# Where the layer norms and their transposes stand in a cross-attention block on one NeuronCore

## The chip, the cores and the metric

The kernel runs on one core of one Trainium2 chip. The metric is the time on the device in microseconds (us), as the median of several runs. Besides these runs there is one execution under the hardware profiler; it has a time of its own, and every duration below is from it.

## What is computed

A cross-attention block in float32: four batches, 512 query rows (`x`) and 512 encoder rows (`ctx`) of 512 features each, 16 heads of 32 features, an MLP of 2048. The mask is all ones.

```python
x = layer_norm(hidden_states, ln1_w, ln1_b)          # (4, 512, 512)
q = x @ q_w + q_b                                    # 16 heads of 32
k = encoder @ k_w + k_b
v = encoder @ v_w + v_b
attn = softmax(where(mask, q k^T / sqrt(32), min))
hidden = (attn v) @ cproj_w + cproj_b + residual
y = gelu(layer_norm(hidden, ln2_w, ln2_b) @ fc_w + fc_b, approximate=True)
out = hidden + y @ proj_w + proj_b
```

## The kernel before

Work is in groups. A group `w` from 0 to 15 is one batch (`w // 4`) and four of its heads (`w % 4`), because four heads of 32 features fill 128 partitions. For a group three products are prepared: K and Q as `[features, rows]` (`prep_k` L196, `prep_q` L206) and V as `[rows, features]` (`prep_v` L218). Each is 4 or 16 matmuls into one PSUM accumulator and a copy out of it by ScalarE (L198, L209, L223); POOL then adds V's bias (L230). After its matmuls each of the three asks for the weights of the group two further on (`load_w`, L189).

Then the group is passed through in four units of 128 query rows. A unit is `scores` (L240, four matmuls into the only `sc` buffer[...]), on VectorE (DVE) a copy with the mask that also takes the minimum (L245), on ScalarE (ACT) the exponential (L249), and `turn`: DVE transposes the exponentials in 32x32 blocks into `tb` (L277). After every second unit DVE appends the reciprocal sums (L282 to L285), and `copies` (L319) moves the 16 blocks of `tb` between partitions by 16 DMAs: this is the exchange, named by group and half. Its target is `pT`, of which there is one, or for some halves the large tiles `gt` or `xe` while they are free. `attend` (L362, `av`) multiplies the exchanged exponentials by V, two or three units after they were made, and DVE divides by the sums into `oT` (L367).

Other tiles matter to the order. `xe` holds a batch's encoder rows (`eT`, loaded by `load_enc`, L150) and its normed and transposed query rows (`xT`). There is one of it, so the next batch's encoder rows can be loaded only when the last V of the batch before has been taken, and `xT` can be overwritten only when its last Q has been. A layer norm is in parts: `x1` loads the rows, `x2` is three parts (statistics of tiles 0 and 1, L116 and L117; of tiles 2 and 3, with the reciprocal root on POOL, L122 and L124; the norm of all four tiles, L128), `x3` is four transposes of the normed tiles through TensorE (L137) with a copy that applies weight and bias, on ACT for even ones (L142) and on DVE for odd ones (L140). `x4` is `load_enc`. The second norm has the same parts (`stat`, `rs`, `norm`, `turns2`). Four accumulators of PSUM (`ps_acc`) are shared by every product, transposes and `av` among them.

The order of all instructions is written out by hand. `first[w]` is a list of pieces of work for group `w`, `later[w]` what may follow from its third unit on. `A(w)` gives the K, Q and V pieces of a group, `C(b)` the output projections (L399), `some(n)` the next n products of the MLP (fc L457, proj L467). The loop over units lays them out by a budget: each piece has a cost (3.4 for a product, 0.5 for a transpose, 0 for the rest), the sum of the group is divided by its four units, and before and after each unit's `turn` as many pieces are taken as the budget allows. So the position of a piece in a list doesn't fix the unit that it falls in, and a pair of transposes can be parted by a unit's scores. Nearly all DMAs, the exchanges among them, are issued by SyncE (SP) in the same order. An issue whose source isn't ready holds back everything that stands behind it.

The last two MLPs have a form of their own (`last_mlps`), which comes after all that is touched here.

Of the kernel before, what the change touches and what calls it, by code (L numbers as in the profile page):

```python
# [74 lines left out]
def xattn_block(ctx: ExitStack, tc: tile.TileContext, x, encT, mask, q_w, k_w, v_w, c_w, fc_w, p_w, vecs, rows, out):  # L75
# [43 lines left out]
    def ln_rs(key):  # L119

        ve = small.tile([P, NT], F32, tag="ve", name=f"ve{key[0]}_{key[1]}")
        nc.gpsimd.tensor_scalar(ve, S["mv", key][:, :, 1], EPS, 1.0, ALU.add, ALU.mult)  # L122
        rs = small.tile([P, NT], F32, tag="rs", name=f"rs{key[0]}_{key[1]}")
        nc.gpsimd.tensor_tensor(rs, ve, nhalf, ALU.pow)  # L124
        S["rs", key] = rs
# [65 lines left out]
    def prep_k(w):  # L191
        b, g = divmod(w, NG)
        kT = kqp.tile([P, L], F32, tag="kT", name=f"kT_{w}")
        acc = acc_tile(f"acck_{w}")
        for d in range(ND):
            nc.tensor.matmul(acc, S["wk", w][:, d, :], eT[:, d, :], start=(d == 0), stop=(d == ND - 1))  # L196
        load_w(w + 2, names=("wk",))
        nc.scalar.activation(kT, acc, AF.Identity, bias=vec[:, KB + g : KB + g + 1], scale=1.0)  # L198
        S["kT", w] = kT

    def prep_q(w):
        b, g = divmod(w, NG)
        qT = kqp.tile([P, L], F32, tag="qT", name=f"qT_{w}")
        acc = acc_tile(f"accq_{w}")
        for d in range(ND):
            nc.tensor.matmul(acc, S["wq", w][:, d, :], xT[:, d, :], start=(d == 0), stop=(d == ND - 1))  # L206
        load_w(w + 2, names=("wq",))

        nc.scalar.activation(qT, acc, AF.Identity, bias=qb[:, g : g + 1], scale=-scale)  # L209
        S["qT", w] = qT  # L210

    def prep_v(w):
        b = w // NG
        v = five.tile([P, NT, P], F32, tag="v", name=f"v_{w}")
        acc = acc_tile(f"accv_{w}")
        for t in range(NT):
            for d in range(ND):
                nc.tensor.matmul(  # L218
                    acc[:, ts(t, P)], eT[:, d, ts(t, P)], S["wv", w][:, d, :],
                    start=(d == 0), stop=(d == ND - 1),  # L220
                )
        load_w(w + 2, names=("wv",))
        nc.scalar.copy(v, acc.rearrange("p (t f) -> p t f", t=NT))  # L223
        S["v", w] = v
        if w:
            v_bias(w)
# [153 lines left out]
    def load_h(b, *ts_):  # L380

        if ("xa", b) not in S:
            S["xa", b] = dram.tile([L, D], F32, tag=f"xa{b}", name=f"xa{b}")
        for t in ts_:
            pool, tag = (hids, "hid") if stays(b, t) else (tiles, "xn")
            S["h", b, t] = pool.tile([P, D], F32, tag=tag, name=f"h_{b}_{t}")
            Q[0].dma_start(out=S["h", b, t], in_=x[b, ts(t, P), :])
            if stays(b, t):
                S["hid", b, t] = S["h", b, t]
# [23 lines left out]
    def stat2(b, t):  # L413
        ln_stat((2, b), t, S["h", b, t])

    def norm2(b, t):
        h = S["h", b, t]
        y = tiles.tile([P, D], F32, tag="xn", name=f"xn2_{b}_{t}") if stays(b, t) else h
        S.setdefault(("yn", b), {})[t] = y
        ln_norm((2, b), t, y, h)  # L420

    def proj_bias(b):
        for t in range(NT):
            if stays(b, t):
                add_row(S["hid", b, t], 1)
# [271 lines left out]
    def do(fn):  # L697
        return [(0.0, fn)]

    def A(w):  # L700
        if w >= NW:
            return []
        return [
            (CHAIN, lambda: prep_k(w)),
            (CHAIN, lambda: prep_q(w)),
            (CHAIN, lambda: prep_v(w)),
        ]

    def C(b):
        return [(CHAIN, lambda t=t: cproj(b, t)) for t in range(NT)]  # L710
# [4 lines left out]
    def turns2(b):  # L715
        return [(TURN, lambda d=d: ln2_turn(b, d)) for d in range(ND)]
# [7 lines left out]
    def inputs(b):  # L724
        ln = [(0.0, lambda part=part: ln1(b, part)) for part in range(3)]
        return do(lambda: load_x(b)), ln, turns1(b), do(lambda: load_enc(b))
# [44 lines left out]
    first = [[] for _ in range(NW)]  # L771
    later = [[] for _ in range(NW)]
    x1, x2, x3, x4 = inputs(1)
    k2, q2, v2 = A(2)
    k3, q3, v3 = A(3)
    k4, q4, v4 = A(4)
    first[0] = [(CHAIN, lambda: prep_v(1)), (CHAIN, lambda: prep_q(1))] + x1 + [k2, q2]
    first[1] = x2[:1] + [v2, k3] + x2[1:2] + [q3] + x2[2:] + [v3] + x4 + x3
    first[2] = [q4, k4, v4] + A(5)[:1]
    first[3] = A(5)[1:] + A(6)  # L780
    mlp = []
    for p in range(NORMAL):
# [2 lines left out]
    def some(n):  # L785
        taken, mlp[:n] = mlp[:n], []
        return taken
# [4 lines left out]
    def h_(b, *ts_):  # L792
        return do(lambda: load_h(b, *ts_))

    def cb(b):
        return do(lambda: c_bias(b))

    def pb_(b):
        return do(lambda: proj_bias(b))

    def rs(b):
        return do(lambda: ln_rs((2, b)))

    def stat(b, *ts_):
        return do(lambda: [stat2(b, t) for t in ts_])

    def norm(b, *ts_):
        return do(lambda: [norm2(b, t) for t in ts_])


    x1, x2, x3, x4 = inputs(2)
    first[3] = x1 + first[3] + cb(0)
    k, q, v = A(7)
    c, t2 = C(0), turns2(0)
    first[4] = [k] + x2[:2] + [q] + x2[2:] + [v] + x3[:2] + x4
    later[4] = c[:1] + x3[2:] + c[1:] + stat(0, 0, 1, 2, 3) + rs(0)
    k, q, v = A(8)
    first[5] = norm(0, 0, 1, 2, 3) + [q] + t2[:2] + [k] + t2[2:] + [v] + pb_(0) + some(5)
    k, q, v = A(9)
    x1, x2, x3, x4 = inputs(3)  # L820
    first[6] = [k, q] + some(5) + [v] + x1
    k, q, v = A(10)
    first[7] = [k, q] + some(6) + [v]

    k, q, v = A(11)
    first[8] = h_(1, 0, 1) + [k] + x2[:1] + [q] + x2[1:2] + some(1) + x2[2:] + [v] + x3 + h_(1, 2, 3) + x4
    later[8] = cb(1) + C(1)
    k, q, v = A(12)
    first[9] = [q] + some(2) + [k] + some(3) + [v]
    k, q, v = A(13)  # L830
    first[10] = [k, q] + some(5) + [v]
    k, q, v = A(14)
    t2 = turns2(1)
# [3 lines left out]
    k, q, v = A(15)  # L837
# [99 lines left out]
```

## Time and profile before

| | us |
|---|---|
| median of 3 runs | 843.63 (842.76 to 844.65) |
| the profiled execution | 839.66 |
| its span, first to last instruction | 837.9 |
| TensorE (PE) busy | 811.3 (97%) |
| DVE / ACT / POOL busy | 562.8 / 348.1 / 91.0 |
| mean granted TensorE clock | 0.986 |

Each row of the profile that is shown below names a line of the kernel, an engine, the operation, the tiles (out<-in), and how many instructions the row merges. In a timeline the first number is the start from the beginning of the span, the second the length, and brackets hold the idle time of the engine just before, with what ended it. In a row of waits the numbers are the total, the count and the longest. A row of a stretch has its ends, its length, the busy time of PE, of the weight loads (PEld), of DVE, ACT and POOL, then the granted clock (1.00 is full), the share of the DMA engines and GB/s. SPq is SyncE's queue of DMA issues.

### The profile page before, as it was taken

To read this page: it belongs to the slowest core of one execution; us is meant where nothing else is said; L and a number is where in the kernel's file an instruction comes from. 1 tells how busy PE (TensorE), PEld (TensorE's weight loads), DVE (VectorE), ACT (ScalarE), POOL (GpSimd) and SP (SyncE) were. 2 spreads that over 40 slices of the span, in tenths; PEclk is the share of its full clock that TensorE was granted. 3 is DMA by queue.
4 is the path that set the end of the run, shared out by engine and by line. 5 is a ranking of instruction groups with operands and counts; after the bars stand their busy time and mean duration, and the time that the engine had idled before them with its cause. 6 is when DMAs were issued, how large, how long until landed. Compare 5 with 4: busy or idle time off the path is not lost.

```text
span 837.9 us, 11898 instructions
## 1 busy us (share of the span) xinstructions
PE 811.3 (97%) x4020; PEld 468.9 (56%) x4020; DVE 562.8 (67%) x1264; ACT 348.1 (42%) x741; POOL 91.0 (11%) x98
## 2 busy tenths in 40 slices
PE   9997799889999998999999999999999999999998
PEld 6544445335445454454545445444446888888887
DVE  3699589685577587756787777688425988168511
ACT  2655364335665553355434657475401331023200
POOL 1010003002000012100012201001021003100011
PEclk9999899899999999999999999999999999999999
DMA  9667869845777775676676966677835551022001
GB/s 335 224 153 190 236 175 229 223 101 129 187 184 191 203 192 149 191 207 171 149 195 188 239 170 160 171 176 170 242 108 175 159 186 41 11 90 76 14 13 38
DMA packets 59740, 134.91 MB, mean 161 GB/s; under 512 B 12144, under 2 KB 14320, under 8 KB 59552
## 3 DMA queue, kind: packets, MB, share of 16 engines
q1 hardware_dynamic: 58416, 130.73, 57.7%
q0 software_dynamic: 736, 2.29, 0.8%
q10 hardware_dynamic: 528, 1.14, 0.5%
q8 instruction: 32, 0.52, 0.3%
q14 instruction: 28, 0.23, 0.1%
HBM read 58.74 MB, written 6.29 MB: 78 GB/s over the span
## 4 chain that ended last, share of the span: by engine, by line
PE 87%; DVE 8%; SPq 2%; DMA 2%; issue 1%; ACT 0%; POOL 0%; DVEq 0%; POOLq 0%; ACTq 0%
PE accf L457 13%; PE accp L467 13%; PE q L561 12%; PE sc L240 7%; PE accc L399 7%; PE av L362 6%; PE acck L196 6%; PE accv L218 5%; PE accq L206 4%; DVE tb L277 3%; DVE s L245 2%; SPq L319 2%; PE tp L137 2%; PE q4p L601 2%; PE q3p L601 2%; PE q5p L601 2%
## 5 line engine op out<-in xcount | busy, mean ns | idle before, releaser
L249 ACT ACTIVATE s<-s,mn 128x512 f32<-128x512 f32 x256 | 181.7, 711 | 143.6 <-DVE mn L245 143.4
L245 DVE CUSTOM_DVE_ANT_0 s<-sc,mb 128x512 f32<-128x512 f32 x256 | 161.4, 686 | 67.8 <-PE sc L240 67.6
L277 DVE STREAM_TRANSPOSE tb<-s 128x512 f32<-128x512 f32 x248 | 161.6, 690 | 8.5 <-ACT s L249 8.5
L457 PE MATMUL accf<-yT,fcw 128*128 128x512 f32 x256 | 115.2, 598 | 0.0
L467 PE MATMUL accp<-pw,gt 128*128 128x512 f32 x256 | 115.1, 599 | 0.0
L467 PEld LDWEIGHTS accp<-pw,gt 128*128 128x128 f32 x256 | 47.2, 190 | 64.5 <-issue 61.1
L457 PEld LDWEIGHTS accf<-yT,fcw 128*128 128x128 f32 x256 | 47.2, 190 | 64.5 <-issue 56.1
L240 PE MATMUL sc<-kT,qT 32*128 32x512 f32 x512 | 74.8, 655 | 2.0 <-DVE mn L245 1.3
L196 PE MATMUL acck<-xe,wk 128*128 128x512 f32 x128 | 61.6, 626 | 6.9 <-DMA xe<-encT_dram 6.9
L218 PEld LDWEIGHTS accv<-wv,xe 128*128 128x128 f32 x512 | 58.9, 192 | 9.4 <-issue 7.9
L218 PE MATMUL accv<-wv,xe 128*128 128x128 f32 x512 | 60.7, 277 | 0.2 <-ACT yT L142 0.2
L561 PE MATMUL q<-ys,gt 128*128 128x256 f32 x256 | 60.2, 379 | 0.0
L206 PE MATMUL accq<-xe,wq 128*128 128x512 f32 x128 | 59.1, 605 | 0.0
L399 PE MATMUL accc<-wc,oT 128*128 128x512 f32 x128 | 56.8, 596 | 0.0
L362 PE MATMUL av<-pT,v 128*32 128x256 f32 x864 | 55.0, 397 | 0.0
L561 PEld LDWEIGHTS q<-ys,gt 128*128 128x128 f32 x256 | 48.6, 190 | 6.6
L230 POOL TENSOR_TENSOR v<-v,row 128x512 f32<-128x512 f32 x16 | 20.3, 1272 | 293.4 <-ACT v L223 293.4
L249 ACT ACT_TABLE_LOAD x22 | 28.2, 1283 | 52.7 <-DVE mn L245 52.7
L249 ACT ACTIVATION_READ_ACCUMULATOR s<-s,mn 128x1 f32 x256 | 47.8, 187 | 0.0
L196 PEld LDWEIGHTS acck<-xe,wk 128*128 128x128 f32 x128 | 24.3, 200 | 40.6 <-issue 28.2
L561 PE MATMUL q<-yT,gt 128*128 128x256 f32 x192 | 46.3, 379 | 0.0
L362 PEld LDWEIGHTS av<-pT,v 128*32 128x32 f32 x864 | 26.0, 113 | 30.2 <-issue 13.3
(117 smaller groups left out, 844.8 us busy)
## 6 DMA issues: line engine op xcount, KB each, us to landing
pT<-tb SPq DMA_DIRECT2D x416, 136.0 KB, 2.4
fcw<-fc_w_dram SPq DMA_DIRECT2D x32, 256.0 KB, 3.1
pw<-p_w_dram SPq DMA_DIRECT2D x32, 256.0 KB, 4.7
gt<-fc_w_dram SPq DMA_DIRECT2D x32, 256.0 KB, 2.7
gt<-tb SPq DMA_DIRECT2D x48, 136.0 KB, 3.1
wk<-k_w_dram SPq DMA_DIRECT2D x16, 256.0 KB, 3.4
xe<-encT_dram SPq DMA_DIRECT2D x16, 256.0 KB, 4.5
wv<-v_w_dram SPq DMA_DIRECT2D x16, 256.0 KB, 3.2
```

Source lines behind the costliest of these rows:

```text
L196: nc.tensor.matmul(acc, S["wk", w][:, d, :], eT[:, d, :], start=(d == 0), stop=(d == ND - 1))
L206: nc.tensor.matmul(acc, S["wq", w][:, d, :], xT[:, d, :], start=(d == 0), stop=(d == ND - 1))
L218: nc.tensor.matmul(acc[:, ts(t, P)], eT[:, d, ts(t, P)], S["wv", w][:, d, :], start=(d == 0), stop=(d == ND - 1),)
L240: nc.tensor.matmul(sc[:, h, :], qT[r, ts(qt, P)], kT[r, :], start=True, stop=True)
L245: nc.vector.tensor_tensor_reduce(out=s, in0=sc[:, h, :], in1=S["mb", w // NG], scale=1.0, scalar=FMAX, op0=ALU.add, op1=ALU.min, accum_out=mn,
L249: nc.scalar.activation(s, s, AF.Exp, bias=mn, scale=-1.0, accum_out=sums[:, qt, h : h + 1])
L277: nc.vector.transpose(tv[:, q, h], S["ps", w, qt][h])
L362: nc.tensor.matmul(av[ts(h, HD), : 2 * P].rearrange(shape, **kw), v[:, t, ts(h, HD)], p[t][h], start=(t == 0), stop=(t == NT - 1),)
L399: nc.tensor.matmul(acc, S["oT", b][:, g, ts(t, P)], wc[:, g, :], start=(g == 0), stop=(g == NG - 1))
L457: nc.tensor.matmul(acc, S["fcw", b, f][:, d, :], S["yT", b][:, d, :], start=(d == 0), stop=(d == ND - 1))
L467: nc.tensor.matmul(acc, gT[q % 2][:, k, ts(t, P)], S["pw", b, q * FQ + k], start=(k == 0), stop=(k == FQ - 1))
L561: nc.tensor.matmul(o, a[:, k], y[:, k], start=(k == 0), stop=(k == 1))
```

## The change

Three things are done to the lists. The statistics of a norm come earlier or its transposes later, so that at least a unit lies between the norm (the last part of `x2`, or `norm`) and its transposes, which stand in pairs. In group 1 V of group 3 is taken ahead of its Q, and the encoder's rows of batch 1 (`x4`) follow directly on that V. In group 4 the encoder's rows stay behind V and the norm goes behind them; the transposes stand between output projections.

```diff
-    first[1] = x2[:1] + [v2, k3] + x2[1:2] + [q3] + x2[2:] + [v3] + x4 + x3
-    first[2] = [q4, k4, v4] + A(5)[:1]
+    first[1] = x2[:1] + [v2, k3] + x2[1:2] + [v3] + x4 + x2[2:] + [q3]
+    first[2] = x3[:2] + [k4] + x3[2:] + [v4, q4] + A(5)[:1]
...
-    first[4] = [k] + x2[:2] + [q] + x2[2:] + [v] + x3[:2] + x4
-    later[4] = c[:1] + x3[2:] + c[1:] + stat(0, 0, 1, 2, 3) + rs(0)
+    first[4] = [k] + x2[:1] + [q] + x2[1:2] + [v] + x4 + x2[2:]
+    later[4] = c[:1] + x3[:2] + c[1:2] + x3[2:] + c[2:] + stat(0, 0, 1, 2, 3) + rs(0)
...
-    first[5] = norm(0, 0, 1, 2, 3) + [q] + t2[:2] + [k] + t2[2:] + [v] + pb_(0) + some(5)
+    first[5] = norm(0, 0, 1, 2, 3) + [q, k] + t2[:2] + [v] + t2[2:] + pb_(0) + some(5)
...
-    first[7] = [k, q] + some(6) + [v]
+    first[7] = [k, q] + x2[:1] + some(3) + x2[1:2] + some(3) + [v]
...
-    first[8] = h_(1, 0, 1) + [k] + x2[:1] + [q] + x2[1:2] + some(1) + x2[2:] + [v] + x3 + h_(1, 2, 3) + x4
+    first[8] = h_(1, 0, 1) + x2[2:] + [k, q] + x3[:2] + some(1) + x3[2:] + [v] + h_(1, 2, 3) + x4
```

What the budget makes of it: in group 2 the first pair of transposes now follows the first unit's scores, in group 5 and in group 8 the second unit's scores part the first pair. The number of instructions on every engine is the same.

## The prediction

> **What bounds the kernel now.** I read the page's busy row and its chain first, then the waits of TensorE, then TensorE's timeline around each wait, then the granted clock after each.
>
> ```profile
> PE 811.3 (97%) x4020; PEld 468.9 (56%) x4020; DVE 562.8 (67%) x1264; ACT 348.1 (42%) x741; POOL 91.0 (11%) x98
> ...
> PE 87%; DVE 8%; SPq 2%; DMA 2%; issue 1%; ACT 0%; POOL 0%; DVEq 0%; POOLq 0%; ACTq 0%
> ...
> PE tp L137 <- DVE xn L128: 10.0, 5, 4.0
> PE acck L196 <- DMA xe<-encT_dram: 6.9, 1, 6.9
> PE tp L137 <- ACT v L223: 2.4, 1, 2.4
> PE sc L240 <- DVE mn L245: 1.3, 2, 0.7
> ```
>
> TensorE sets the time: it is idle for 26.6 us of 837.9, and 19.3 us of that are transposes that wait for a norm or a copy (12.4) and a K product that waits for the encoder's rows (6.9). All lie at four places, the layer norms that the change touches:
>
> ```profile
> 68.46 1.47 PE L137 MATMUL tp<-ident,xn 128*128 128x128 f32 x12
> 72.34 0.66 PE L137 MATMUL tp<-ident,xn 128*128 128x128 f32 x4 [2.41 <-ACT v L223]
> 72.93 2.09 PE L240 MATMUL sc<-kT,qT 32*128 32x512 f32 x8
> ...
> 81.10 1.14 PE L240 MATMUL sc<-kT,qT 32*128 32x512 f32 x8
> 89.14 5.79 PE L196 MATMUL acck<-xe,wk 128*128 128x512 f32 x8 [6.89 <-DMA xe<-encT_dram]
> ```
>
> ```profile
> 151.37 2.61 PE L137 MATMUL tp<-ident,xn 128*128 128x128 f32 x8 [3.95 <-DVE xn L128]
> 153.91 3.64 PE L362 MATMUL av<-pT,v 128*32 128x256 f32 x32
> ...
> 184.94 2.70 PE L137 MATMUL tp<-ident,xn 128*128 128x128 f32 x8 [3.33 <-DVE xn L128]
> 187.43 4.36 PE L196 MATMUL acck<-xe,wk 128*128 128x512 f32 x8
> ```
>
> The reader is to see two things: the idle time in brackets, and that the work behind it is long. A K product takes 3.63 elsewhere and 5.79 at 89.14; scores 1.07 and 2.09; the attention product 1.87 and 3.64. The stretches by the granted clock (the number after PE, PEld, DVE, ACT and POOL) say why:
>
> ```profile
> 72.34:76.00 3.66, 3.66 (x14) 1.47 (x15) 3.59 (x8) 1.29 (x2) 1.27 (x1) 0.58 0.44 132
> ...
> 89.14:94.94 5.80, 5.80 (x12) 2.31 (x12) 0.00 (x0) 0.00 (x0) 0.00 (x0) 0.63 0.99 288
> 151.37:157.50 6.13, 6.13 (x44) 2.81 (x44) 2.03 (x4) 0.78 (x1) 0.00 (x0) 0.50 0.80 263
> ```
>
> So "busy" hides a second loss. With full-clock durations (chain of 8: 3.6; V product 3.7; av 1.87; sc 1.07; 8 transposes 0.87) the surplus is about 3.9 us at the first place, 3.7, 2.4 and 2.4 at the others. Idle and surplus together are about 33 us, the ceiling of any such change.
>
> The encoder's rows are late because the queue is busy:
>
> ```profile
> 59.68 10.75 SPq L319 DMA_DIRECT2D gt<-tb  x16
> ...
> 74.33 10.98 SPq L319 DMA_DIRECT2D pT<-tb  x16
> 85.41 0.53 SPq L189 DMA_DIRECT2D wv<-v_w_dram  x1
> 85.98 1.88 SPq L150 DMA_DIRECT2D xe<-encT_dram  x4
> ...
> 137.90 10.21 SPq L319 DMA_DIRECT2D pT<-tb  x16
> ```
>
> **The change part by part.** No instruction is added or removed; the order on each engine moves. I lay each place out in the times of before, an earlier gain shifting the later ones whole.
>
> Batch 1 (groups 1 and 2). V of group 3 comes ahead of its Q: 57.48 to 61.25, av to 63.1, scores when DVE lets them go, at 63.7 as before, to 64.8, then Q of group 3 to 68.4. The next scores need DVE's last minimum of the scores before, which ends at 70.6 (DVE's order up to there doesn't change: norms 65.98 to 67.8, minima 68.11 to 70.6). So TensorE stands for 2.3 us again: the wait for the V copy (2.41) is replaced, not removed. Scores and the first 8 transposes end at 72.7 (74 at half clock). SP is free of the exchange at 70.43, then wk 0.6, wv 0.5: the encoder's rows are asked for at 71.6, not 85.98. Their landing took 3.1 us for the first, so K of group 4 starts at 74.7 and stands for about 1 to 2 us. I take it at the slow 5.7 of its row: 80.5. Then av, scores, 8 transposes, V (7.5), and scores, Q, av, scores (7.65), with 0.5 for a clock still low: K of group 5 at 96.1 against 102.64. Gain 6.5. Ends: 9 at full clock, 4.5 if the last row's landing (5.5) and a longer slow stretch add.
> The exchange that now follows the encoder's rows isn't delayed: DVE has its sums ready at 74.3, the four requests end at 73.5. Wq of group 5 moves from 71.17 to behind that exchange, 85.4; it is needed at 100. The next exchange (gt) starts when DVE is done, about 89.7, issues for 11.3, lands about 2.4 later, at 103; its av comes at 104. That cover is 1 us, the thinnest; if it is gone, TensorE stands there.
>
> [...]
>
> Batch 2 (group 4). After V of group 7, at 147.35, av comes first. It needs the exchange issued from 137.90: the last of 16 leaves at 147.5 and lands 2.5 (median of its rows) later, at 150.0. So 3.95 us of wait for the norm become 2.65 of wait for the exchange, and the clock will fall again: I take 2.0 of surplus, between 1.7 (after the 2.41 stop) and 3.7 (after 3.95). Then av, scores, 4 output projections, 16 transposes in two pairs, scores, av: 21.9. Scores of group 5 start at 147.35+2.65+2.0+21.9 = 173.9 against 176.84. Gain 2.9; ends 1.3 and 5.0. Half of the statistics now stand behind the exchange's sums on DVE, and the root on POOL before the V bias. The norms end near 155.3 (four at 0.47, 0.7 more beside POOL's bias); the transposes want them at 158.
>
> The second norm of batch 0 (group 5). The norms end 9.4 us after the scores start (176.84 to 186.2), DVE being behind with statistics. TensorE has scores, Q and now K ahead: 8.1. The stop falls from 3.33 to 1.2, too short, I take it, for the clock to fall. But the planner's budget splits the pair: scores stand between the first and second set of transposes, and on DVE the copy of the second (L140) falls behind minima 2.5, transposes 2.4 and sums 0.9: it ends at 17.1. The first fc needs it for its second quarter at 16.4: a new stop of 0.7. The next av starts at 19.8 against 24.06. Gain 4.2; ends 2.5 and 5.
>
> Batch 3 (group 8). The statistics move into group 7, where DVE is busy 61 of 96 us: 4 of 0.8 us, hidden; without cover, 3.2. The norms follow the first transposes of group 8 and end at 303.9+4x0.47 = 305.8 (they took 0.96 beside POOL's row additions, which are not there now). TensorE wants them at 305.2: stop 0.6. Scores, one set, a proj, two sets: 311.9; V waits 0.4 for ACT's copy of its bank; V, av, scores: 319.0 against 323.66. Gain 4.6; ends 2.5 and 5.2.
>
> Sum 6.5+2.9+4.2+4.6 = 18.2. The profiled execution took 839.66 (span 837.9): 821.5 after. The median of the runs is 3.97 above it; kept, that gives 825.4.
>
> [...] The row has 0.58 after 2.41 us, and 0.65 from 317.3 to 322 after three stops of 0.53, 1.13 and 1.07. I go by the row.
>
> **The rivals.** [...] (2) Exchanges become the bound of groups 2 to 4. The queue needs 2 x 10.9 + 1.5 + 1.9 us of issue in a group, 25.2 of the 29.0 that group 2 keeps (scores at 70.7 to the next group's at 99.7). One exchange took 13.73 (from 122.46, behind the x loads); if the two of groups 2 and 3 do too and av waits 2 us each at four places, 8 of the gain are gone: 833. (3) Slower: the same queue, worse. With e us more for each exchange and a slack of 3.8 in a group, groups 2 to 4 lose 3 x (2e - 3.8); the 18.2 are gone from e = 4.9, an exchange of 15.8 us, and at 17 us it is 850. Against it: no row is above 13.73. (4) Nothing: the stops only change their names (batch 1 and 2 do so in part), 843. Against it: 6.9 us of encoder wait have no successor in any queue.
>
> **How the numbers follow.** Likeliest 0.62 (825.4, its own range 821 to 830), clock 0.13, exchanges 0.15, slower 0.07, nothing 0.03. From 818 to 834 holds the first three: 0.8 with what the bounds leave out. A measurement can tell 0.2% (1.7 us) from no change. Faster 0.9, same 0.03, slower 0.07.
>
> **What would show it.** K of group 4 starting near 75 with a stop of 1 to 2 instead of 6.9; scores of group 2 waiting 2.3 for DVE; av of group 3 waiting about 2.6 for its exchange with a clock near 0.6 behind it; a short stop of the first fc for L140; no transposes above 1.2 us of wait. I am wrong if av waits for exchanges in groups 2 to 4, or if the clock is low in stretches where it was 1.00 before.

## The result and the profile after

| | before | after |
|---|---|---|
| median of the runs, us | 843.57 (842.76 to 844.65) | 823.96 (822.55 to 825.83) |
| ratio, 95% interval | | 0.9768 (0.9741 to 0.9796) |
| profiled execution, us | 839.66 | 822.63 |
| its span, us | 837.9 | 820.5 |
| TensorE busy, us | 811.3 (97%) | 803.1 (98%) |
| mean granted TensorE clock | 0.986 | 0.998 |

The change takes 19.6 us, 2.3%, off the time. In the span of the profiled executions it is 17.4, and of these 8.2 are busy time of TensorE: the same 4020 matmuls ran at a higher clock (0.998 granted against 0.986). The other 9.2 are idle time. The profiled execution of the changed kernel is one with a high clock: the other three had 0.995 to 0.996.

The profile page of the changed kernel, the row of busy time, the chain that ended last, and the waits of TensorE (total, count, longest):

```profile
PE 803.1 (98%) x4020; PEld 465.9 (57%) x4020; DVE 563.1 (69%) x1264; ACT 348.0 (42%) x741; POOL 90.6 (11%) x98
...
PE 91%; DVE 5%; SPq 2%; DMA 1%; issue 1%; ACT 0%; POOL 0%; DVEq 0%; POOLq 0%; ACTq 0%
...
PE sc L240 <- DVE mn L245: 3.8, 3, 2.7
PE acck L196 <- DMA xe<-encT_dram: 3.2, 1, 3.2
PE av L362 <- DMA wv<-v_w_dram: 1.7, 1, 1.7
PE accf L457 <- DVE yT L140: 1.5, 1, 1.5
PE tp L137 <- DVE h L400: 0.5, 1, 0.5
```

The waits of transposes for norms (10.0) and for the copy of V (2.4) are gone. In their place stand scores that wait for DVE's minimum, an attention product, and an fc product: smaller stops with new names. What the attention product waits for needs care. It is labelled with V's weights, but `av` reads `pT`, and the exchange that fills it had just been issued on the same queue. I read it as the wait for that exchange.

The timeline of TensorE in the changed kernel, at the four places in order (start, length, what it is, idle time before it and what ended it):

```profile
57.60 3.84 PE L218 MATMUL accv<-wv,xe 128*128 128x128 f32 x32
...
71.26 1.14 PE L240 MATMUL sc<-kT,qT 32*128 32x512 f32 x8 [2.66 <-DVE mn L245]
72.33 1.09 PE L137 MATMUL tp<-ident,xn 128*128 128x128 f32 x8
76.66 5.36 PE L196 MATMUL acck<-xe,wk 128*128 128x512 f32 x8 [3.23 <-DMA xe<-encT_dram]
...
97.11 3.70 PE L196 MATMUL acck<-xe,wk 128*128 128x512 f32 x8
...
143.65 1.93 PE L362 MATMUL av<-pT,v 128*32 128x256 f32 x32 [1.75 <-DMA wv<-v_w_dram]
145.51 1.14 PE L240 MATMUL sc<-kT,qT 32*128 32x512 f32 x8
...
166.31 1.14 PE L240 MATMUL sc<-kT,qT 32*128 32x512 f32 x8
...
174.42 1.70 PE L137 MATMUL tp<-ident,xn 128*128 128x128 f32 x4
...
184.74 2.84 PE L457 MATMUL accf<-yT,fcw 128*128 128x512 f32 x6 [1.54 <-DVE yT L140]
187.52 1.93 PE L362 MATMUL av<-pT,v 128*32 128x256 f32 x32
...
283.76 1.14 PE L240 MATMUL sc<-kT,qT 32*128 32x512 f32 x8
...
299.30 3.84 PE L218 MATMUL accv<-wv,xe 128*128 128x128 f32 x32 [0.43 <-ACT xe L142]
...
306.00 7.13 PE L399 MATMUL accc<-wc,oT 128*128 128x512 f32 x16
```

The reader is to see that of these only the K product behind the encoder's rows (5.36) ran at a low clock: 0.68 granted over its length. The scores behind the 2.66 stop take their usual 1.14, and the attention product at the second place its usual 1.93, where it took 3.64 before; both had the clock at 1.00. The four transposes of 1.70 had it at 1.00 too: they follow the norms as these are done.

Each place has a stretch between two points that occur in both traces, so its gain can be read off. The ends of the stretches in the kernel before:

```profile
57.48 3.70 PE L206 MATMUL accq<-xe,wq 128*128 128x512 f32 x8
...
102.64 3.70 PE L196 MATMUL acck<-xe,wk 128*128 128x512 f32 x8
...
176.84 1.14 PE L240 MATMUL sc<-kT,qT 32*128 32x512 f32 x8
...
200.82 1.93 PE L362 MATMUL av<-pT,v 128*32 128x256 f32 x32
...
297.07 1.14 PE L240 MATMUL sc<-kT,qT 32*128 32x512 f32 x8
...
323.50 7.03 PE L399 MATMUL accc<-wc,oT 128*128 128x512 f32 x16
```

| place | stretch | before | after | gain | predicted |
|---|---|---|---|---|---|
| batch 1, groups 1 and 2 | first product behind the scores at 56.4 (Q of group 3 before, V of group 3 after) to K of group 5 | 45.16 | 39.51 | 5.65 | 6.5 |
| batch 2, group 4 | end of V of group 7 (where the stop begins) to scores of group 5 | 29.42 | 24.41 | 5.0 | 2.9 |
| second norm of batch 0, group 5 | those scores to the next `av` | 23.98 | 21.21 | 2.8 | 4.2 |
| batch 3, group 8 | scores of group 8's first unit to its first output projection | 26.43 | 22.24 | 4.2 | 4.6 |

The sum is 17.6, against 17.4 in the span. Each figure is one execution against one. How much a single pair can be off is seen at a stop that b_only, c_only and d_only below leave as it was: K of group 4 waited 6.89 us for its rows in the profile of before, and 8.0, 7.8 and 8.5 in theirs.

### The profile page after: what moved, and what is told of

Read it like the earlier page. It is cut to its first block, busy times and chain, and to the rows that moved or that the text cites. A ratio compares the mean times of both kernels' runs of the same rounds, so it can differ in the third digit from the quotient of the medians.

```text
span 820.5 us, 11894 instructions
## 1 busy us (share of the span) xinstructions
PE 803.1 (98%) x4020; PEld 465.9 (57%) x4020; DVE 563.1 (69%) x1264; ACT 348.0 (42%) x741; POOL 90.6 (11%) x98
## 3 DMA queue, kind: packets, MB, share of 16 engines
q10 hardware_dynamic: 528, 1.14, 0.6%
## 4 chain that ended last, share of the span: by engine, by line
PE 91%; DVE 5%; SPq 2%; DMA 1%; issue 1%; ACT 0%; POOL 0%; DVEq 0%; POOLq 0%; ACTq 0%
PE accp L467 14%; PE accf L457 14%; PE q L561 12%; PE sc L240 8%; PE av L362 7%; PE accc L399 6%; PE acck L196 6%; PE accv L218 6%; PE accq L206 6%; DVE s L245 2%; PE q4p L601 2%; PE q3p L601 2%; PE q7p L601 2%; PE q6p L601 2%; PE q2p L601 2%; PE q1p L601 2%
## 5 line engine op out<-in xcount | busy, mean ns | idle before, releaser
L240 PE MATMUL sc<-kT,qT 32*128 32x512 f32 x512 | 73.0, 640 | 4.6 <-DVE mn L245 3.8
L362 PE MATMUL av<-pT,v 128*32 128x256 f32 x864 | 52.2, 382 | 1.7 <-DMA wv<-v_w_dram 1.7
(117 smaller groups left out, 841.5 us busy)
```

The source lines that it names most:

```text
L240: nc.tensor.matmul(sc[:, h, :], qT[r, ts(qt, P)], kT[r, :], start=True, stop=True)
L362: nc.tensor.matmul(av[ts(h, HD), : 2 * P].rearrange(shape, **kw), v[:, t, ts(h, HD)], p[t][h], start=(t == 0), stop=(t == NT - 1),)
```

## The experiments

The theory at the start: each of the four places gives its own part, about as the table has it; what is gained is idle time plus the slow clock behind it. Rival theories: the encoder's rows alone carry the first place; the clock, not the waits, makes the gain; the gains of single places are swallowed by the next exchange. Beside each set of experiments the kernel before was timed anew, at 841.1 to 841.5 us; only ratios are compared.

### One place at a time

Each kernel has the changed lists of one place on the kernel before: `first[1]`, `first[2]`; `first[4]`, `later[4]`; `first[5]`; `first[7]`, `first[8]`.

```diff
# a_only: first[1], first[2]   b_only: first[4], later[4]   (new lines of the change)
# c_only: first[5]             d_only: first[7], first[8]
```

> Only the lists of groups 1 and 2 are changed. Theory (each place pays for its own stop, later work shifts whole): TensorE's stop of 6.9 us for the encoder's rows becomes 3.2, the surplus behind it stays near 1.7, the chain to the K product of group 5 is 5.7 shorter, and the other three places lose what they lost before; 843.6 - 5.7 = 837.9 us. Rival (SyncE's queue is what bounds groups 2 to 4, and what is gained here is given back at the next exchange): the attention products of groups 2 and 3 wait for their exchanges and the time stays above 841.

> Only the lists of group 4 are changed. Theory: 3.95 us of stop become about 1.75 (for the exchange), and the slow clock behind it (3.7 us of surplus) goes or stays with the stop's length: 838.6 us when the clock stays up, as in the changed kernel (5.0 less), 840.7 when it falls as my prediction had it. Rival (queue): the exchange of group 3 lands later than in the changed kernel and the attention product waits as long as the transposes did, 843.

> Only the list of group 5 is changed. Theory: the stop of 3.33 us and the surplus of 2.4 are replaced by about 1.2 of transposes paced by the norm and 1.5 of the first fc waiting for DVE's copy; 2.9 less than before, 840.7 us. My prediction's size was 4.2, 839.4. Rival (the norm's lateness comes from group 4's order, so that the edit here gains nothing by itself): 843.

> Only the lists of groups 7 and 8 are changed. Theory: three stops (2.7 us together) and the surplus behind them go but for 0.4; 4.3 less, 839.3 us; DVE's norms of tile 0 to 3 take 0.47 us each instead of 0.96 because POOL is idle beside them. Rival (the statistics cost in group 7 what they save in group 8): 842.5, with waits of scores for DVE in group 7.

| kernel | median, us | ratio to before (841.2) | gain from the ratio |
|---|---|---|---|
| a_only | 835.54 | 0.9925 (0.9905 to 0.9944) | 6.3 |
| b_only | 839.68 | 0.9981 (0.9962 to 1.0001) | 1.6 |
| c_only | 838.24 | 0.9957 (0.9941 to 0.9974) | 3.6 |
| d_only | 836.86 | 0.9940 (0.9925 to 0.9954) | 5.0 |

The gains add to 16.5 us, 1.97%. The whole change has 2.32% (2.04 to 2.59), so within the uncertainty of the four they add up. With the first place alone no attention product waits for an exchange, so its gain isn't swallowed there. Group 4 alone is the weakest, and its interval touches no change. TensorE's timeline at its stop:

```profile
150.92 2.70 PE L362 MATMUL av<-pT,v 128*32 128x256 f32 x32 [2.02 <-DMA wv<-v_w_dram]
153.55 2.01 PE L240 MATMUL sc<-kT,qT 32*128 32x512 f32 x8
```

The stop for the exchange is 2.02, and the clock falls behind it (granted 0.63), where the whole change has 1.75 and a granted clock of 1.00. That is part of the reason, not all: in this profile the stretch of the table is still 25.41, a gain of 4.0. The profiled execution took 837.09, and the nine of this kernel go from 836.21 to 842.08; where the others lost more isn't known.

### The two halves of the first place

First the encoder's rows alone: V ahead of Q and the rows' issues behind V, with the four transposes in one block where they were.

```diff
-    first[1] = x2[:1] + [v2, k3] + x2[1:2] + [q3] + x2[2:] + [v3] + x4 + x3
+    first[1] = x2[:1] + [v2, k3] + x2[1:2] + [v3] + x4 + x2[2:] + [q3] + x3
```

> Of groups 1 and 2 only V of group 3 goes ahead of its Q, with the encoder's rows behind it; the transposes of batch 1 stay in one block ahead of the scores of group 2. Theory (the encoder's rows are what counts): K of group 4 stops about 2 us for its rows instead of 6.9, because the transposes fill some of the wait, and the transposes wait for no copy, only for the norm; 837 to 839 us, as with the whole edit of groups 1 and 2. Rival (the distance between norm and transposes counts): 842.

Then the transposes alone: the encoder's rows asked for where they were, the transposes in pairs in group 2.

```diff
-    first[1] = x2[:1] + [v2, k3] + x2[1:2] + [q3] + x2[2:] + [v3] + x4 + x3
-    first[2] = [q4, k4, v4] + A(5)[:1]
+    first[1] = x2[:1] + [v2, k3] + x2[1:2] + [q3] + x2[2:] + [v3] + x4
+    first[2] = x3[:2] + [k4] + x3[2:] + [v4, q4] + A(5)[:1]
```

> Of groups 1 and 2 only the transposes of batch 1 move, into group 2 behind its first scores; Q of group 3 stays ahead of V, the encoder's rows are asked for behind the exchange as before. Theory (encoder's rows count): the wait of 2.4 us for the V copy goes, and the K product then waits longer for rows that land no earlier than before, at 89; 843 to 844 us. Rival (distance counts): 839 to 840.

The rows alone took 833.43 us, ratio 0.9906 (0.9892 to 0.9921): no worse than the whole place (0.9925). The transposes alone took 847.55, ratio 1.0078 (1.0063 to 1.0093): slower than before. The timelines of TensorE, with the rows alone and then with the transposes alone:

```profile
73.39 0.90 PE L137 MATMUL tp<-ident,xn 128*128 128x128 f32 x4 [3.12 <-ACT qT L209]
74.22 2.09 PE L240 MATMUL sc<-kT,qT 32*128 32x512 f32 x8
...
83.21 3.70 PE L196 MATMUL acck<-xe,wk 128*128 128x512 f32 x8
...
94.61 3.70 PE L196 MATMUL acck<-xe,wk 128*128 128x512 f32 x8
```

```profile
71.54 2.09 PE L240 MATMUL sc<-kT,qT 32*128 32x512 f32 x8 [2.06 <-DVE mn L245]
...
89.27 6.70 PE L196 MATMUL acck<-xe,wk 128*128 128x512 f32 x8 [13.99 <-DMA xe<-encT_dram]
```

With the rows alone Q of group 4 stands between the transposes and K of group 4, which finds its rows in place: no stop, and 3.70 us, the length of K of group 5 as well. With the transposes alone K comes ahead of Q, and so 14 us ahead of its rows. So at this place the early request, with V ahead of Q as it needs, carries the gain. The later transposes bring K of group 4 forward, and don't pay even together with it. From the same scores of group 1 (56.90 and 56.89) K of group 5 starts at 94.61 with the rows alone and at 97.87 with the whole place, because there K of group 4 stands for 3.63 us and runs slowly (5.35). The medians differ the same way, by 2.1 us, but their intervals overlap.

### Is it the stop or the clock?

28 (and, in the changed kernel, 13) products of the identity with itself are put ahead of K of group 4, to keep TensorE at work while it waits; their result is read by nothing.

```diff
+    def fill(n):
+        def go():
+            acc = acc_tile("fill")
+            for _ in range(n):
+                nc.tensor.matmul(acc[:, :P], ident, ident, start=True, stop=True)
+        return [(0.0, go)]
...
+    k4 = (CHAIN, lambda plain=k4[1]: (fill(28)[0][1](), plain()))   # 13 on the changed kernel
```

> The kernel before, with 28 products of the identity with itself ahead of the K product of group 4, into an accumulator that nobody reads: about 6 us of work in the stop of 6.9 us. It measures the slow clock by itself. Theory (the surplus behind a stop is the clock and is worth what the profile says): the K product takes 3.7 us instead of 5.8, and the time is 841.4, 2.2 less. Rival (the K product is slow because its operand is still landing): it still takes 5 us or more with the clock at 1.00, and the time is that of before, 843.6.

> The changed kernel, with 13 such products ahead of the same K product, in its stop of 3.2 us. Theory: the K product takes 3.7 us instead of 5.4, 822.3 us. Rival: 824.0, with a K product of 5 us at full clock; and if products in the stop push the next scores, up to 825.

On the kernel before it is 841.53 us, ratio 1.0008 (0.9993 to 1.0022): nothing. TensorE's timeline:

```profile
73.50 0.66 PE L137 MATMUL tp<-ident,xn 128*128 128x128 f32 x4 [2.41 <-ACT v L223]
74.08 1.14 PE L240 MATMUL sc<-kT,qT 32*128 32x512 f32 x8
...
90.55 2.81 PE L196 MATMUL acck<-xe,wk 128*128 128x512 f32 x6 [2.15 <-DMA xe<-encT_dram]
94.09 1.12 PE L196 MATMUL acck<-xe,wk 128*128 128x512 f32 x2 [0.73 <-DMA xe<-encT_dram]
```

K now takes 3.93 us (2.81 and 1.12) and gains little: it has to stop twice, for one part of the rows and for the last. Counted from the scores of group 1 (at 56.41 and 57.57) it ends at 37.6 us instead of 38.5. The 5.79 us that K took before were a slow clock (granted 0.63) that for the most part covered the rows' own landing. So of the 2.2 us of surplus that the prediction counted at that K 0.9 were to be had by a faster clock between these two profiles, and the time shows none of it. On the changed kernel it is 824.64, ratio 0.9800 (0.9786 to 0.9815), against 0.9768 without: nothing gained. K runs at 3.60 instead of 5.36 there, but in that profile the scores and transposes ahead of it were slow (1.63 and 1.97 instead of 1.14 and 1.09), and the attention product that waits for the exchange of group 3 stopped for 2.51 and then took 3.44.

### Pieces taken back from the changed kernel, and its last stops

First, on the changed kernel, the block of four transposes of the rows-alone kernel.

```diff
-    first[1] = x2[:1] + [v2, k3] + x2[1:2] + [v3] + x4 + x2[2:] + [q3]
-    first[2] = x3[:2] + [k4] + x3[2:] + [v4, q4] + A(5)[:1]
+    first[1] = x2[:1] + [v2, k3] + x2[1:2] + [v3] + x4 + x2[2:] + [q3] + x3
+    first[2] = [q4, k4, v4] + A(5)[:1]
```

> The changed kernel with one thing taken back: in the first place, V still ahead of Q and the encoder's rows still asked for there, but all four transposes of batch 1's first norm stand in one block again, ahead of the scores of group 2. If the place's gain is the early rows alone and the moved transposes cost about 2 us (as the two separate edits say: 835.5 against 833.4), this is about 822; if the moved transposes pay once the other places are changed too, 826 or more. In the trace: no stop for the encoder's rows, one stop of about 3 us of the transposes for the copy of Q, and K of group 5 at about 94.6 us instead of 97.1.

It took 821.54 us, ratio 0.9772 (0.9756 to 0.9789): the same as the changed kernel (0.9768). The first part of the expectation held, K of group 5 starts at 94.33 instead of 97.11. But TensorE's timeline in it says where these 2.8 us went:

```profile
94.33 3.70 PE L196 MATMUL acck<-xe,wk 128*128 128x512 f32 x8
...
142.13 3.44 PE L362 MATMUL av<-pT,v 128*32 128x256 f32 x32 [3.02 <-DMA wv<-v_w_dram]
145.50 1.14 PE L240 MATMUL sc<-kT,qT 32*128 32x512 f32 x8
```

The scores start at 145.50; in the changed kernel they start at 145.51. All of it was lost within one attention product: a stop of 3.02 instead of 1.75, and 3.44 of work instead of 1.93. SyncE's queue shows a part of the reason. The changed kernel, then the one with the block:

```profile
103.14 11.44 SPq L319 DMA_DIRECT2D pT<-tb  x16
...
115.25 1.89 SPq L155 DMA_DIRECT2D xn<-x_dram  x4
...
117.72 11.28 SPq L319 DMA_DIRECT2D gt<-tb  x16
...
130.70 10.03 SPq L319 DMA_DIRECT2D pT<-tb  x16
```

```profile
100.35 10.50 SPq L319 DMA_DIRECT2D pT<-tb  x16
...
113.98 12.76 SPq L319 DMA_DIRECT2D gt<-tb  x16
...
128.44 10.03 SPq L319 DMA_DIRECT2D pT<-tb  x16
```

From 103.14 to 140.73 one request follows the other with pauses of about 0.1 us: three exchanges, the rows of batch 2's norm, and weights. With the block the same requests run from 100.35 to 138.47, again without a pause. They begin 2.8 us earlier and end 2.3 earlier; the last exchange lands more slowly (4.2 us for the median of its 16 requests instead of 3.6), so that its consumer could start 1.5 earlier; and the slow clock (granted 0.64 from 142.13 to 146.50, where the changed kernel has 1.00) took these 1.5. So the queue and the landing kept back 1.3 of the 2.8 us and the clock the rest. In the kernels where group 4 is the old one this exchange is not what is waited for, and there the gain is kept: up to the transposes of batch 2 the rows alone stay 3.3 us ahead of the whole place.

Next, the copies of the second norm's transposes exchanged between ScalarE and VectorE for batch 0.

```diff
-        if d % 2:
+        if d % 2 != (key == (2, 0)):
             nc.vector.tensor_scalar(dst[:, d, :], tp, wd, bd, ALU.mult, ALU.add)
```

> The changed kernel with the copies of the second norm of batch 0 exchanged between the engines: the first and third block of 128 channels on VectorE, the second and fourth on ScalarE. If the 1.54 us stop of the first fc product is because VectorE has the copy of the second pair behind other work, the stop goes or falls below 0.7 and the kernel is 1 to 1.5 us faster than the changed one (822.5 to 823); if ScalarE is as late, or the stop comes from the norms behind it, nothing changes (824).

It took 823.47 us, ratio 0.9791 (0.9776 to 0.9806), no different from the changed kernel (0.9768; the intervals overlap). The stop of the fc product fell from 1.54 to 0.90, not below the 0.7 that was expected: of each pair one copy is still VectorE's. And in this profile the stop for the exchange was 2.46 instead of 1.75, with `av` at 2.73 and scores at 1.98 behind it (granted clock 0.63). So the stop does hang on VectorE's copies, and the gain is too small to be seen in the time. The stop comes with the edit of group 5 alone: c_only has it at 1.54 too.

Then the first output projection put ahead of the attention product that waits for the exchange.

```diff
-    first[4] = [k] + x2[:1] + [q] + x2[1:2] + [v] + x4 + x2[2:]
-    later[4] = c[:1] + x3[:2] + c[1:2] + x3[2:] + c[2:] + stat(0, 0, 1, 2, 3) + rs(0)
+    first[4] = [k] + x2[:1] + [q] + x2[1:2] + [v] + x4 + c[:1] + x2[2:]
+    later[4] = x3[:2] + c[1:2] + x3[2:] + c[2:] + stat(0, 0, 1, 2, 3) + rs(0)
```

> The changed kernel with the first output projection of batch 0 put into the list of group 4 ahead of the second half of its transposes' exchange, so that the output of V times the exchanged numbers starts later by one product. If the 1.75 us stop of that output is the exchange landing late, it goes and the kernel is about 1.7 us faster (822.3), more (to 4) where the clock would have fallen behind the stop; if the exchange is itself moved later by the product, the stop stays and nothing is gained (824).

It took 827.82 us, ratio 0.9844 (0.9827 to 0.9861): 0.8% slower than the changed kernel, which neither side of the expectation had. The stop for the exchange did go, but the norm (`x2[2:]`), which I had left behind the projection in the list, slipped behind the next scores on DVE. TensorE's timeline, then DVE's:

```profile
147.22 1.14 PE L240 MATMUL sc<-kT,qT 32*128 32x512 f32 x8
153.94 2.60 PE L137 MATMUL tp<-ident,xn 128*128 128x128 f32 x8 [5.58 <-DVE xn L128]
156.34 4.86 PE L399 MATMUL accc<-wc,oT 128*128 128x512 f32 x8
```

```profile
150.88 2.49 DVE L277 STREAM_TRANSPOSE tb<-s 128x512 f32<-128x512 f32 x4
153.29 1.88 DVE L128 TENSOR_SCALAR xn<-xn,mv,rs 128x512 f32<-128x512 f32 x4
```

That is the change taken back at this one place: no unit between the norm and its transposes. DVE comes to the norm only behind the minima and the block transposes of a unit, TensorE stands for 5.58 us, and the slow clock (granted 0.66 over the transposes and the projection) adds 1.6 at the transposes (2.60 for 1.04) and 1.3 at the projection (4.86 for 3.60). That is 8.4, less the 1.75 that went, 6.7; the ratios differ by 0.76%, 6.4 us. So this is the price of the missing unit at this place, and a test of the change itself.

Last, the three together.

> All three of these on the changed kernel: the first place's transposes in one block again, the copies exchanged, the output projection ahead. If they are additive, 824 less 2, 1.3 and 1.7: about 819; if the stops only move to the next exchange, 822 to 824.

It took 825.55, ratio 0.9815 (0.9800 to 0.9830), with the same 5.6 us stop for the norm. It can't say whether the other two add up. No version was measurably better than the changed kernel.

## Why the prediction was right, and where it was off

The median was put at 825.4 and is 823.96, and the likeliest case is the one that came. Step by step:

**Batch 1, 6.5 predicted, 5.65 measured.** The mechanism was right. The stop of the scores for DVE came as predicted, 2.66 for 2.3. The encoder's rows were asked for at 72.13 (71.6). The mis-sized term is their landing: K started 4.5 us after the request, not 3.1, and stood for 3.23, not 1 to 2. K's 5.36 is near the 5.7 taken, and the 0.5 kept for a low clock afterwards wasn't needed. That this place's gain is the early request is shown by the two halves. The prediction gave no share to the two; the moved transposes alone made the kernel slower. The exchange behind the encoder's rows cost nothing, as predicted: it was issued in 10.27 us. In the kernel before, the exchange directly behind these rows took 11.28 to issue, and the one from 46.68, with none ahead of it, 10.26. The first four requests of the one in the changed kernel did land late, 5.0 us after their issue against 2.4 in the median of the kernel, but the attention product that needs it came at 94.18 without a stop.

**Batch 2, 2.9 predicted, 5.0 measured.** The replaced wait is there, 1.75 for 2.65. The step that failed is "the clock will fall again: I take 2.0 of surplus": in the profile of the changed kernel `av` and scores had a granted clock of 1.00. The stop was 0.9 shorter than reckoned as well, and the chain from `av` to the scores of group 5 took 22.66 instead of 21.9. With a stop of 2.02, 2.46, 2.51 and 3.02 in b_only, in the exchanged copies, behind the 13 products and in the block of four, `av` and scores were slow by 1.6, 1.6, 1.5 and 1.5. So the 2.0 was not far off for a stop behind which the clock falls, and the profile of the changed kernel is the lucky one. By itself the place gave 1.6 in the medians and 4.0 in its profile.

**Second norm of batch 0, 4.2 predicted, 2.8 measured.** The norm paces the first set of transposes (1.70 for four, 0.66 for the second set) as predicted. That the clock wouldn't fall for the stop of 1.2 left there was an estimate; the transposes of 1.70 had it at 1.00. The stop of the first fc product came at its place, for L140, but was 1.54, not 0.7; the clock behind it was 1.00. The mis-sized term is DVE's sums, taken as 0.9. DVE's timeline of the changed kernel, then POOL's:

```profile
182.31 1.21 DVE L284 COPY rr<-rsum 128x256 f32<-128x256 f32 x1
```

```profile
182.10 1.26 POOL L230 TENSOR_TENSOR v<-v,row 128x512 f32<-128x512 f32 x1 [12.27 <-ACT v L223]
```

The copy takes 0.29 in the median of its 31. Here it begins 0.21 us behind POOL's V bias, ends 0.16 behind it, and takes 0.92 more. The prediction had reckoned with POOL beside the norms, but not beside this copy.

**Batch 3, 4.6 predicted, 4.2 measured.** V waits 0.43 for ACT's copy (0.4). The stop of 0.6 for the norm didn't come as a stop; a first set of 1.10 for four transposes, at a granted clock of 1.00, is what is left of it.

The errors have both signs and cancel: 17.6 for 18.2. That the sum fits so well is luck. The median fell 1.4 lower than predicted because the profiled execution stands 3.97 below the median of before but only 1.33 below that of after; keeping 3.97 was the largest single error of the sum. (The ceiling of 33 us is 31.7 by its own terms, 19.3 of idle time and 12.4 of surplus.)

**The rivals.** "Clock", put at 0.13, is the case that TensorE keeps its clock behind the stops that are left. No run shows a length up to which a stop leaves the clock up: the rows of the kernel before have a granted clock of 0.58 behind 2.41 us and of 0.65 behind stops of 0.53, 1.13 and 1.07, and in the changed kernel it was 1.00 behind two of the stops (2.66, 1.75) and 0.68 behind the third (3.23, with K at 5.36). So the mean clock of 0.998 is not this case's proof. "Exchanges become the bound" happened where it was put, in groups 2 to 4, but at one place and for 1.75 us instead of four times 2; it became visible when the first place was sped up by 2.8 us more and the time showed none of it. "Nothing" and "slower" are out by the interval.

## What to carry to other kernels

Between a producer on the slower engine and its consumer on the bounding one, leave a unit of the consumer's other work, and look at where the producer really stands in its own engine's order: one list entry moved behind a product cost 6.4 us here. It isn't a rule for every place: at the first one the early request carried all of the gain, and the distance alone made the kernel slower, since it brought forward a product whose rows weren't there. So where one place has two edits, separate them. Before a further stop is attacked, look at what its consumer waits for next: here 2.8 us gained ahead of a full queue were 1.5 at its end, and a fall of the clock took these.

## What the runs showed of the hardware

- **The length of a stop alone doesn't decide whether the clock falls.** Five profiles (before, b_only, c_only, d_only, and before with the 28 products, which come later) have the same instructions up to the stop of 2.41 us ahead of group 2's scores, and the same stop. The granted clock from these scores to the end of Q, in before, d_only and the kernel with the products:

```profile
72.93:79.24 6.31, 6.31 (x17) 2.30 (x17) 6.24 (x16) 3.56 (x10) 0.71 (x1) 0.73 0.67 166
73.83:78.69 4.86, 4.86 (x17) 1.67 (x16) 4.79 (x13) 2.12 (x6) 0.71 (x1) 1.00 0.66 156
74.08:78.94 4.86, 4.86 (x17) 1.67 (x16) 4.79 (x13) 2.12 (x6) 0.71 (x1) 1.00 0.56 137
```

  In b_only and c_only the two took 6.35 and 6.36 us at 0.73. So whether the clock fell differed from execution to execution, and where it fell it cost the same 1.5 us. Behind 2.66 us the scores took 1.14 in the changed kernel and 1.63 in that with 13 products, again ahead of these. Of the stops at the exchange, 1.75 kept the clock (1.00), and 2.02, 2.46 and 3.02 lost it (0.63, 0.63 and 0.64); behind 2.51 `av` took 3.44 instead of 1.93. Of the stops for the encoder's rows, four between 3.14 and 3.63 all gave a K product of 5.35 to 5.37. Why equal stops end differently is not shown by any run here.
- **Slow work can hide a late transfer.** K at 5.79 us, and K at 3.93 us with two stops of 2.15 and 0.73, ended within 0.9 us of each other, and the times differ by 0.08% (-0.07 to 0.22).
- **A copy of VectorE beside a POOL addition** took 1.21 us instead of 0.29. It isn't stretched evenly: in the changed kernel, in c_only, with the 13 products and with the exchanged copies it began about 0.2 us (0.12 in the last) behind the addition and ended 0.15 to 0.16 behind its end. In b_only it began 0.23 ahead of the addition and took 0.29.
- **A queue that issued without a pause for 37.6 us** passed on 2.3 of 2.8 us gained ahead of it. Moving the norm's 1.9 us of row loads to another queue would be the next thing to try; it wasn't tried.
